# Two attention layers on one core: the first pair of heads, one ordering instruction earlier, one product later, one table load earlier

## The chip, the cores and the metric

The kernel runs on one core of one Trainium2 chip. The time is the device time of the whole program in microseconds (us), as the median of several runs. All data are 32-bit floats.

## What is computed

The input x has 4 images of 32x32 positions and 768 channels. Two layers are applied, each `x = x + attention(groupnorm(x))`. Cut to one layer (the second has biases on q, k and v, and tables for 14x14 positions that are clamped outside):

```
xn  = (x - mean) / sqrt(var + eps)         # 32 groups of 24 channels, no scale or shift
q, k, v = split(xn @ Wqkv)                 # 12 heads of 64
bias[query, key] = q . Rh[hq - hk] + q . Rw[wq - wk]
attn = softmax(scale * q k^T + bias)       # 1024 x 1024 for each head and image
x   = x + (attn @ v) @ Wproj + bproj
```

## The kernel before, in words

**Tiling.** Channels lie on the 128 partitions, six chunks of them (`NC`), positions on the free axis, 1024 (`S`) in two halves of 512. Two heads make a pair: head 0 of the pair uses rows 0 to 63 of TensorE's array, head 1 rows 64 to 127. There are 8 images (4 for each layer) with 6 pairs each, so 48 pairs `g`. A pair has 8 units `n` of 128 queries each. A unit (g, n) makes the scores of 128 queries against 1024 keys for both heads.

**One unit's chain.** `biases` (L513) adds the two position terms on GpSimd into a tile `sc` (two instructions, one for each head). `scores` (L527) is four matmuls of 64x512 on TensorE into PSUM. `exponentials` (L540) adds the bias on VectorE with the row minimum (L546) and takes exp with the row sum on ScalarE (L550). `divide` (L555) takes a reciprocal on VectorE (L558), which has to wait until both exps have ended, and multiplies on ScalarE (L564) or, for one head in units 2 and 4, on GpSimd (L562). `turn` (L566) transposes on VectorE (L570), writes to DRAM, and a later read brings the transposed tile back as `pt`. `weigh` (L586) multiplies with the values. Six `sc` tiles exist, so the biases of unit n + 3 wait for the transposes of unit n. PSUM holds two score tiles (the two heads of one unit) and two tiles of 1024 for everything else.

**The products for the next pair.** While pair g runs, q and k of pair g + 1 are made by four products G0 to G3 (`products`, L347), and values for two pairs at a time by four products of kinds 0 to 3 (`values`, L409); two of these four are made in each pair, under the names V0 and V1. They are a block product with seven multiplications in place of eight, so sums and differences of tiles and of weights (on GpSimd: `combine`, L130, `combine_values`, L141, `sums`, L296) come ahead of them and VectorE additions behind.

**Crossed halves.** A product other than kind 3 is written in two halves (`crossed`, L332). In the first half head-row group 0 takes one operand and group 1 the other, in the second half they change over. Between the halves stands an ordering instruction (`Crossed.between`, L325): a reduction over one column of a weight tile onto itself on VectorE (L330), or a copy on ScalarE (L328). It reads and writes what the first half has read and the second half will read, so it waits for the first half, and the second half waits for it. It computes nothing new. Kind 3 (G3, L369; the value product of kind 3, L426) has no halves and no ordering instruction.

**Order.** The order on every engine is the order of the Python calls; each engine takes its own instructions strictly in that order. The loop over units (L828) puts into unit (g, n): the ordering instructions that are held, the biases of unit n + 2, the scores and exponentials of unit n + 1, the transposes of unit n, the reciprocal of unit n + 1 and its multiplications, and between them the products that the plan names for n (L820 to L824, `run_part`, L885). A first half that was begun puts its product into `held`; its ordering instruction comes at the next unit, except in units 2 and 6.

**The front.** Before the loop (L775 to L819) stand the norm of image 0 (`norm_first`, L214: sums over groups, a square root on ScalarE at L232, the normalization of twelve half chunks, alternately on VectorE, L241, and ScalarE, L239), all four products of q and k for pair 0, the value products of kinds 0 and 3 (V0 at L799, V1 at L808), the position terms (`positions`, L461; `place_positions`, L485, writes them to DRAM; `diagonals`, L498, reads them back skewed, eight DMAs for each half of the queries), then biases, scores, exponentials and the division of unit (0, 0), and the first half of G0 for pair 1, whose ordering instruction comes as the first thing of unit (0, 0). In pair 0 the DMAs of head 1 in `diagonals` are issued by ScalarE's queue (L506), all others by SyncE's.

Of the kernel before, what the change touches and what calls it, by code (L numbers as in the profile page):

```python
# [56 lines left out]
def attention_blocks(ctx: ExitStack, tc: tile.TileContext, a: dict, out: bass.AP):  # L57
# [156 lines left out]
    def norm_first():  # L214

        mv = mv_of[0]
        w = small.tile([P, 2, NC], FP, tag="nrm", bufs=2, name="nrm_work")
        nrm = small.tile([P, NC, 2], FP, tag="nrm", bufs=2, name="nrm_0")
        total = ps_m.tile([P, 2, HALF], FP, tag="m", name="groups_0")[:, :, 0]
        work = nrm.rearrange("p c s -> p (c s)")  # L220
        part, mean, inv, shift = (work[:, k : k + 1] for k in range(4))
        off, var = w[:, 0, :], w[:, 1, :]
        nc.vector.tensor_reduce(part, mv[:, :, 0], mybir.AxisListType.X, ALU.add)
        nc.tensor.matmul(total[:, 0:1], lhsT=same_group, rhs=part, start=True, stop=True)
        nc.vector.tensor_scalar(mean, total[:, 0:1], 1.0 / GS, None, ALU.mult)
        nc.vector.tensor_scalar(off, mv[:, :, 0], mean, None, ALU.subtract)
        nc.vector.tensor_tensor(var, off, off, ALU.mult)
        nc.vector.tensor_tensor(var, var, mv[:, :, 1], ALU.add)
        nc.vector.tensor_reduce(part, var, mybir.AxisListType.X, ALU.add)
        nc.tensor.matmul(total[:, 1:2], lhsT=same_group, rhs=part, start=True, stop=True)  # L230
        nc.vector.tensor_scalar(inv, total[:, 1:2], 1.0 / GS, EPS, ALU.mult, ALU.add)
        nc.scalar.activation(part, inv, AF.Sqrt)  # L232
        nc.vector.reciprocal(inv, part)
        nc.vector.tensor_scalar(shift, mean, inv, -1.0, ALU.mult, ALU.mult)

        def apply(c, h, scalar):
            x = xn_of[0][h][c]
            if scalar:
                nc.scalar.activation(x, x, AF.Identity, bias=shift, scale=inv)  # L239
            else:  # L240
                nc.vector.tensor_scalar(x, x, inv, shift, ALU.mult, ALU.add)  # L241

        return apply
# [254 lines left out]
    def diagonals(g, i):  # L498
        td = t_of[g]
        for h in range(2):  # L500
            for y in range(4):
                src = bass.AP(
                    td.tensor, td.offset + (4 * i * P + HW * y) * P + h * 2 * HW + HW - 1,
                    [[P - 1, HW], [P * P, 4], [1, HW]],
                )
                (nc.scalar if h and not g else nc.sync).dma_start(  # L506
                    out=rel_of[g, i][y * HW : (y + 1) * HW, h, 1, :, :], in_=src
                )

# [45 lines left out]
    def divide(g, n):  # L555
        st = st_of[g, n]
        last = g + 1 == NPAIR
        nc.vector.reciprocal(st[:, 2, :], st[:, 1, :])  # L558
        for h in range(2):
            sc = sc_of[g, n, h].rearrange("p k j -> p (k j)")  # L560
            if h == 0 and n in (2, 4) and not last:
                nc.gpsimd.tensor_scalar(sc, sc, st[:, 2, h : h + 1], 1.0, ALU.mult, ALU.mult)  # L562
            else:
                nc.scalar.mul(sc, sc, st[:, 2, h : h + 1])  # L564
# [209 lines left out]
    with tc.manual_schedule(engines=ENGINES):  # L774
# [30 lines left out]
            combine_values(0, stage)  # L805
        load_w(1, "a")
        now["G3"].part()
        now["V1"].part()  # L808
        positions(0, 1)()
        run(later)  # L810
        run(later)
# [1 line left out]
        fetch(3)  # L813
        biases(0, 0)
        scores(0, 0)()
        divide(0, 0)
        biases(0, 1)
        ahead["G0"].part()
        held = [ahead["G0"]]  # L819
        same = {  # L820
            0: ("O1 previous", "G0", "V0"), 4: ("G1", "G3", "G2"), 5: ("G2", "O0"),
            7: ("O0", "O1", "G0 next"),
        }
        plans = {**same, 1: ("V0", "V1"), 3: ("V1", "G1")}, {**same, 1: ("V0",), 3: ("G1", "V1")}  # L824
        before = {}

        units = [(g, n) for g in range(NPAIR) for n in range(NT)]
        for at, (g, n) in enumerate(units):  # L828
            im, pair = divmod(g, NP)
            end = im + 1 == NI  # L830
            if n == 0:
                now = dict(ahead) if g + 1 < NPAIR else {}
                ahead = prepare(g + 2) if g + 2 < NPAIR else {}
                if g + 1 < NPAIR:
                    now.update(out_groups(g))
                now["O1 previous"] = before.get("O1")
                now["G0 next"] = ahead.get("G0")
                before = now
                if pair == 3 and not end:
                    stages, apply = norm(im + 1)  # L840
                todo = []
                if g + 1 == NPAIR:
                    fetch_last()
                    todo = put_out(im, 0, range(8, 12)) + put_out(im, 1, range(12))
                    todo += put_out(im, 2, range(0, 12, 2))
            shares = [0, 3, 0, 4, 4, 3, 0, 4]
            if (pair, n) in loads and not end:
                load_x(im + 1, loads[pair, n], 0)
            if pair == 4 and n in (1, 2) and not end:
                for c in range(3 * n - 3, 3 * n):  # L850
                    load_x(im + 1, c, 1)
            if im + 1 < B:
                if pair == 0 and n < NC:
                    load_x(im + 1, n, 0, 1)
                c = n - 2 if pair == 0 else loads.get((pair, n - 2), loads.get((pair - 1, n + 6), -1))
                if pair < 3 and c >= 0:
                    stats(im + 1, c, 1 if pair == 0 else 0, xn_of[im + 1][0][c])
            if n == 3 and 0 < g + 1 < NPAIR - 1:
                later.append(lambda: load_w(g + 2, "a"))
            for group in held if n not in (2, 6) else ():  # L860
                group.between()
            if n not in (2, 6):
                held = []
            run(early)
            early, later = later, early
            if at + 2 < len(units):
                biases(*units[at + 2])
            exps = scores(*units[at + 1]) if at + 1 < len(units) else None
            if n == 7:
                placing = []  # L870
            if n == 7 and g + 1 < NPAIR:
                placing.append(positions(g + 1, 1))
            if exps:
                exps()
            if n in (2, 7):
                run(placing)
            run(behind[0])
            behind.append(behind.pop(0))
            if pair == 3 and n in stages and not end:
                stages[n]()  # L880
            pieces = [now[name] for name in plans[pair % 2].get(n, ()) if now.get(name)]
            if n == 0 and len(pieces) == 2:
                pieces.insert(0, None)

            def run_part(k):  # L885
                if k < len(pieces) and pieces[k]:
                    group = pieces[k]
                    started = group.parts is not None
                    group.part()
                    if not started and group.last is not None:  # L890
                        held.append(group)

            run_part(0)
            turn(g, n)
            done = 2 if n == 0 else len(pieces) if n == 1 or (n, pair % 2) == (3, 0) else 1
            for k in range(1, done):
                run_part(k)
            if n == 1:
                placing = [positions_of() for positions_of in early_positions]
                early_positions.clear()  # L900
            if (n, pair % 2) == (3, 0):
                for group in held:
                    group.between(scalar=True)
                held = []
            if at + 1 < len(units):
                divide(*units[at + 1])
            if n in (0, 1) and g + 1 < NPAIR:
                combine(g + 1, n)
            if n in (3, 5) and pair % 2 and g + 1 < NPAIR:
                combine_values(g + 1, n // 4)  # L910
            if pair == 4 and not end:
                for h, c in applies.get(n, ()):
                    apply(c, h)
            if not end:
                for which, c in sum_steps.get((pair, n), ()):
                    sums(im + 1, which, c)
            if (n, pair % 2) == (3, 1):
                for group in held:
                    group.between()
                held = []  # L920
            for k in range(done, len(pieces)):
                run_part(k)
            take(todo, shares[n])
            if n == 6:
                weigh(g, (0, 1))
            elif n == 2 and g:
                weigh(g - 1, (2, 3))
# [63 lines left out]
```

## Time and profile before

| What | us |
|---|---|
| Median of 3 runs | 3318.47 |
| Lowest and highest of them | 3314.69, 3321.06 |
| The profiled execution, its own time | 3317.58 |
| Its span, first to last instruction | 3315.3 |
| TensorE busy in it | 3270.6 (99%) |
| VectorE busy | 2549.7 (77%) |
| GpSimd busy | 2386.5 (72%) |
| ScalarE busy | 1999.1 (60%) |

In the views of the profile PE is TensorE's matmuls, PEld its weight loads, DVE VectorE, ACT ScalarE, POOL GpSimd, SP SyncE; a q behind the name is the engine's queue of control instructions and DMA issues. Times count from the start of the span. A row of the timeline has the start, the duration, the engine, the line and the operation, the tiles (out<-in) and the shape, the count, and in brackets the idle time of the engine before it with what ended it. The tile `pj` is the PSUM tile of a q/k product, `pv` of a value product, `tp` of a position product, `s` of scores, `av` of values weighed, `sm` the sums of a softmax. A 32-bit matmul is recorded as two; so a half of a q/k product is x12, and a half of a value product x48.

### The profile page before, as it was taken

To read this page: it belongs to the slowest core of one execution; us is meant where nothing else is said; L and a number is where in the kernel's file an instruction comes from. 1 tells how busy PE (TensorE), PEld (TensorE's weight loads), DVE (VectorE), ACT (ScalarE), POOL (GpSimd) and SP (SyncE) were. 2 spreads that over 40 slices of the span, in tenths; PEclk is the share of its full clock that TensorE was granted. 3 is DMA by queue.
4 is the path that set the end of the run, shared out by engine and by line. 5 is a ranking of instruction groups with operands and counts; after the bars stand their busy time and mean duration, and the time that the engine had idled before them with its cause. 6 is when DMAs were issued, how large, how long until landed. Compare 5 with 4: busy or idle time off the path is not lost.

```text
span 3315.3 us, 64963 instructions
## 1 busy us (share of the span) xinstructions
PE 3270.6 (99%) x25060; PEld 1882.7 (57%) x25060; DVE 2549.7 (77%) x4091; ACT 1999.1 (60%) x2996; POOL 2386.5 (72%) x1259
## 2 busy tenths in 40 slices
PE   7999999999999999999999999999999999999998
PEld 4566555655555555555555555655555555655554
DVE  5887778877787877777777777777777777777775
ACT  3676655566556665566655666566656567565653
POOL 6877866679676796667867778677786777767762
PEclk9999999999999999999999999999999999999999
DMA  4999899899998998899989999899998999898987
GB/s 134 329 343 316 315 339 330 316 336 322 331 318 316 329 330 307 317 328 319 334 308 316 330 321 329 313 327 316 334 322 304 338 317 331 311 327 299 329 287 269
DMA packets 524180, 1047.38 MB, mean 316 GB/s; under 512 B 139104, under 2 KB 202080, under 8 KB 474720
## 3 DMA queue, kind: packets, MB, share of 16 engines
q1 hardware_dynamic: 470976, 1015.84, 86.1%
q10 hardware_dynamic: 52896, 27.40, 2.8%
q8 instruction: 198, 3.24, 0.4%
q14 instruction: 110, 0.90, 0.1%
HBM read 568.00 MB, written 475.09 MB: 315 GB/s over the span
## 4 chain that ended last, share of the span: by engine, by line
PE 90%; DMA 5%; DVE 2%; POOL 1%; issue 1%; SPq 0%; ACT 0%; ACTq 0%; DVEq 0%; POOLq 0%
PE pj L341 21%; PE s L534 19%; PE av L599 18%; PE oo L341 13%; PE pv L341 11%; PE pj L369 3%; DMA td<-tb 3%; PE tp L472 2%; PE pv L426 2%; DMA pt<-td 1%; DMA xn<-in_x 1%; DVE tb L570 1%; PE o L678 1%; POOL sc L520 1%; DVE st L209 0%
## 5 line engine op out<-in xcount | busy, mean ns | idle before, releaser
L520 POOL TENSOR_TENSOR sc<-rel 128x1024 f32<-128x1024 f32 x768 | 1879.4, 2481 | 473.1 <-DVE tb L570 454.9
L546 DVE CUSTOM_DVE_ANT_0 sc<-s,sc 128x1024 f32<-128x1024 f32 x768 | 910.9, 1223 | 353.1 <-PE s L534 288.3
L564 ACT ACTIVATE sc<-sc,sm 128x1024 f32<-128x1024 f32 x674 | 743.5, 1144 | 643.2 <-DVE sm L558 494.5
L550 ACT ACTIVATE sc<-sc,sm 128x1024 f32<-128x1024 f32 x768 | 878.5, 1146 | 350.5 <-DVE sm L546 349.0
L570 DVE STREAM_TRANSPOSE tb<-sc 128x1024 f32<-128x1024 f32 x768 | 908.1, 1223 | 59.6 <-DMA td<-tb 55.7
L534 PE MATMUL s<-k,q 64*128 64x512 f32 x3072 | 738.8, 596 | 2.8 <-DVE sm L546 2.7
L599 PE MATMUL av<-pt,v 128*64 128x256 f32 x6144 | 686.2, 381 | 10.3 <-DMA pt<-td 9.0
L599 PEld LDWEIGHTS av<-pt,v 128*64 128x64 f32 x6144 | 436.7, 137 | 289.2 <-issue 49.2
L341 PE MATMUL oo<-attn,wo 64*128 64x512 f32 x2112 | 475.3, 589 | 0.0
L534 PEld LDWEIGHTS s<-k,q 64*128 64x128 f32 x3072 | 284.0, 187 | 302.7 <-issue 268.7
L562 POOL TENSOR_SCALAR sc<-sc,sm 128x1024 f32<-128x1024 f32 x94 | 105.9, 1127 | 374.9 <-DVE sm L558 374.9
L341 PEld LDWEIGHTS oo<-attn,wo 64*128 64x128 f32 x2112 | 201.1, 187 | 227.8 <-issue 226.9
L341 PEld LDWEIGHTS pv<-wv,xn 64*128 64x128 f32 x4608 | 271.6, 188 | 35.2 <-issue 25.1
L341 PE MATMUL pv<-wv,xn 64*128 64x128 f32 x4608 | 274.1, 272 | 1.0 <-DVE wv L330 1.0
L341 PE MATMUL pj<-xn,wa 64*128 64x512 f32 x1152 | 268.2, 596 | 5.1 <-DVE wa L330 3.5
L341 PE MATMUL pj<-xn,w 64*128 64x512 f32 x1152 | 263.4, 589 | 0.0
L341 PE MATMUL pj<-s,w 64*128 64x512 f32 x576 | 262.7, 589 | 0.6 <-DVE v L443 0.6
L341 PE MATMUL pj<-s,wc 64*128 64x512 f32 x576 | 262.7, 589 | 0.0
L341 PEld LDWEIGHTS pj<-xn,wa 64*128 64x128 f32 x1152 | 113.5, 189 | 140.5 <-issue 125.5
L341 PEld LDWEIGHTS pj<-xn,w 64*128 64x128 f32 x1152 | 112.5, 187 | 134.8 <-issue 132.9
L443 DVE TENSOR_TENSOR v<-pv,v 128x512 f32<-128x512 f32 x216 | 140.2, 686 | 61.0 <-ACT v L445 44.0
L495 ACT COPY rel<-raw 32x256 f32<-32x256 f32 x384 | 155.0, 404 | 11.3 <-DMA part<-res 3.4
(93 smaller groups left out, 2642.0 us busy)
## 6 DMA issues: line engine op xcount, KB each, us to landing
td<-tb SPq DMA_DIRECT2D x384, 1024.0 KB, 6.3
pt<-td SPq DMA_DIRECT2D x382, 1024.0 KB, 8.8
tdr<-t ACTq DMA_DIRECT2D x96, 256.0 KB, 6.2
part<-res SPq DMA_DIRECT2D x84, 256.0 KB, 4.4
res<-part SPq DMA_DIRECT2D x84, 256.0 KB, 4.8
wa<-in_wqk SPq DMA_DIRECT2D x48, 384.0 KB, 3.1
wc<-in_wqk SPq DMA_DIRECT2D x48, 384.0 KB, 6.9
wv<-in_wv SPq DMA_DIRECT2D x24, 768.0 KB, 12.6
```

The lines of the kernel that those rows point to most:

```text
L341: nc.tensor.matmul(to, lhsT=w, rhs=x, start=at == half == 0, stop=at == 0 and half == 1)
L369: nc.tensor.matmul(t[:, h, :], lhsT=w[rows, c, :], rhs=x[c][rows, :], start=(c == 0), stop=(c == NB - 1),)
L443: add = lambda to, x, y: nc.vector.tensor_tensor(to, x, y, ALU.add)
L495: nc.scalar.copy(rel[rows, :, 0, :, :], raw[rows, :, :, WIDE - 1 - HW - y : WIDE - 1 - y])
L520: nc.gpsimd.tensor_tensor(sc.rearrange("p (a k) (u l) -> p a (k u) l", a=4, l=8), rel[:, h, 0, m, :].unsqueeze(1).unsqueeze(3).to_broadcas ...
L534: nc.tensor.matmul(ps[h][:, cols], lhsT=q[rows, n * P : (n + 1) * P], rhs=k[rows, cols], start=True, stop=True,)
L546: nc.vector.tensor_tensor_reduce(out=sc, in0=ps[h], in1=sc, scale=-scale, scalar=BIG, op0=ALU.add, op1=ALU.min, accum_out=st[:, 0, h : h + 1],
L550: nc.scalar.activation(sc, sc, AF.Exp, bias=st[:, 0, h : h + 1], scale=-1.0, accum_out=st[:, 1, h : h + 1],)
L562: nc.gpsimd.tensor_scalar(sc, sc, st[:, 2, h : h + 1], 1.0, ALU.mult, ALU.mult)
L564: nc.scalar.mul(sc, sc, st[:, 2, h : h + 1])
L570: nc.vector.transpose(tb[:, :, h, :], sc_of[g, n, h])
L599: nc.tensor.matmul(av[rows, at * 2 * P : (at + 1) * 2 * P], lhsT=v_of[g][:, k, rows], rhs=pt_of[g, quarter].rearrange("p n r k h i -> p (n ...
```

## The change

Five edits, all in the front or in pair 0:

1. In `norm_first`, behind the last step of the norm, one exponential of one column (`part` from `shift`, with scale 0). It brings ScalarE's load of the table of exponentials to this place; the result is not used.
2. In `diagonals`, the four DMAs of head 1 for the second half of the queries of pair 0 go to SyncE's queue; those of the first half stay on ScalarE's.
3. The value product of kind 3 for pair 0 leaves the front and goes into unit (0, 0), behind G0, under the name V3.
4. G0 of pair 1, first half, and its ordering instruction now both stand in front of the division of unit (0, 0), so in front of its reciprocal on VectorE.
5. The value products of pair 0's loop move one slot: V0 from units 0 and 1 to 1 and 2, V1 from 1 and 3 to 2 and 3. Unit (0, 2) no longer leaves out the ordering instruction.

```diff
         nc.vector.tensor_scalar(shift, mean, inv, -1.0, ALU.mult, ALU.mult)
+        nc.scalar.activation(part, shift, AF.Exp, scale=0.0)
...
-                (nc.scalar if h and not g else nc.sync).dma_start(
+                (nc.scalar if h and not g + i else nc.sync).dma_start(
...
         now["G3"].part()
-        now["V1"].part()
         positions(0, 1)()
...
         scores(0, 0)()
+        ahead["G0"].part()
+        ahead["G0"].between()
         divide(0, 0)
         biases(0, 1)
-        ahead["G0"].part()
-        held = [ahead["G0"]]
+        held = []
...
-        before = {}
+        first_plan = {
+            **same, 0: ("G0", "V3"), 1: ("V0",), 2: ("V0", "V1"), 3: ("V1", "G1"),
+        }
+        before = {"V3": now["V1"]}
...
-                now["O1 previous"] = before.get("O1")
+                now["O1 previous"], now["V3"] = before.get("O1"), before.get("V3")
...
-            for group in held if n not in (2, 6) else ():
-                group.between()
-            if n not in (2, 6):
+            if n not in (2, 6) or at == 2:
+                for group in held:
+                    group.between()
                 held = []
...
-            pieces = [now[name] for name in plans[pair % 2].get(n, ()) if now.get(name)]
+            pieces = [now[name] for name in (plans[pair % 2] if g else first_plan).get(n, ()) if now.get(name)]
```

The number of matmuls, of activations of full size, of transposes and of DMAs stays; one activation of one column is added. Behind pair 0 the order is that of before.

## The prediction, made before the changed kernel was run

> **What bounds the kernel now.** I read the page's busy shares first, then the waits of TensorE, then the chain of work and the timeline in the front, where all five edits lie.
>
> ```profile
> span 3315.3 us, 64963 instructions
> PE 3270.6 (99%) x25060; PEld 1882.7 (57%) x25060; DVE 2549.7 (77%) x4091; ACT 1999.1 (60%) x2996; POOL 2386.5 (72%) x1259
> ```
>
> TensorE is busy for all but 45 us, so only work or idle time of TensorE can be won. The loop behind the front is not touched; what TensorE is ahead at the end of pair 0 it keeps, if nothing else is late. Where does it idle in the front? The timeline of PE:
>
> ```profile
> 55.33 2.15 PE L534 MATMUL s<-k,q 64*128 64x512 f32 x8
> 60.46 4.54 PE L341 MATMUL pj<-xn,wa 64*128 64x512 f32 x12 [2.97 <-DVE wa L330]
> ...
> 78.79 3.13 PE L534 MATMUL s<-k,q 64*128 64x512 f32 x8 [1.43 <-DVE sm L546]
> 82.91 2.95 PE L341 MATMUL pv<-wv,xn 64*128 64x128 f32 x48 [0.99 <-DVE wv L330]
> ```
>
> Second half of G0 for pair 1: 2.97 us idle for the ordering instruction, then 4.4 us (60.46 to 64.83, where the next product starts) for what takes 2.57 elsewhere (52.76 to 55.33). The table by stretch says why the half was slow (the column 0.50 is the granted clock):
>
> ```profile
> 61.40:64.70 3.30, 3.30 (x10) 1.39 (x8) 3.30 (x6) 3.01 (x5) 0.69 (x1) 0.50 0.33 127
> ```
>
> The clock was halved behind the idle time. So this stall cost 2.97 + 1.8 = 4.8 us. The chain of work shows what led to it:
>
> ```profile
> 51.88 2.31 DMA tdr<-t
> 54.22 0.36 ACTq L506
> ...
> 56.05 1.28 ACT L550
> 57.35 2.38 ACT sc L550 x4
> 59.79 0.46 issue
> 60.25 0.16 DVE wa L330
> ```
>
> ScalarE waits for the write of the position terms, issues four DMAs, loads the table of exponentials (1.28), does both exps; then comes the reciprocal, and only behind it on VectorE the ordering instruction, though its product's first half ended at 55.33.
>
> [...] half clock for 3.41 us after 2.97 idle. [...] The load is 1283 here[...] (the exp follows at 57.35, and the 2.08 us ahead of the load hold the DMA issues). [...] Identity and copies run behind exps without another load. [...] Here that is 4 x 0.45 = 1.8 us of ScalarE.
>
> **The change, step by step** (times of before's span, start cost left out until the end). I carry rows forward with before's durations: a q/k half product 2.57, a value half product 2.7, scores 1.72, position products 0.9; on VectorE a pair of L546 2.35, transposes 2.3; 0.2 from the end of a product to VectorE.
>
> *V3 leaves the front.* In before it ran from 47.39 to 50.14. Now the position products run from 47.4 to 48.3. Scores (0,0) need the last addition to k, which ends at 49.04 (47.62 + 1.42): V3 hid that, now PE idles 0.8. Scores 49.1 to 50.85, first half of G0 to 53.4, scores (0,1) to 55.2.
>
> *Ordering instruction.* VectorE does the L546 of (0,0) from 51.15 to 53.5, then the ordering instruction at 53.65 (0.2 after the half product). The second half of G0 follows the scores without idling: 55.25 to 57.8. The stall and the halved clock go. The wait that it adds: the reciprocal stands behind it. But the reciprocal is due only after the exps, and those: position copies from 48.5 to 51.2, no DMAs, no table, exps 52.35 to 54.85. Nothing is late by it. V3 then 57.8 to 60.6.
>
> *What is late next is VectorE.* From scores (0,1), at 55.5: L546 2.4, transposes (0,0) 2.3, addition to q 1.1, reciprocal 0.15, V3's two additions 1.4 (moved here), L546 of (0,2) 2.35: 65.1. Then transposes 2.3, reciprocal 0.1, statistics (L209) 0.65; the ordering instruction of V0 at 68.2 to 68.35. PE meanwhile: scores (0,2) to 62.3, V0's first half to 65.0, position products to 65.9, scores (0,3) to 67.6. It idles 0.8, and V0's second half runs from 68.4 to 71.1. V1's first half needs a PSUM tile; in the built order it takes that of the position products, free by 67.3, not that of V0. To 73.8; scores (0,4) to 75.5. VectorE: L546 of (0,3) to 70.65, V0's additions 71.3 to 73.2, transposes to 75.5, reciprocal, statistics, ordering instruction 76.25 to 76.4. PE idles 0.95; V1's second half 76.45 to 79.1.
>
> Before, V1's second half ended at 85.69, where G1 starts; from there both kernels have the same order, and before had no further idle time up to 107.7. **Gain: 85.69 - 79.13 = 6.6 us.** As a check, the losses that go: 2.97 + 1.8 + 1.43 + about 1.2 (the 3.13 of the scores) + 0.99 = 8.4, less new ones of 0.8 + 0.8 + 0.95 = 2.55, leaves 5.9; 0.7 are small gaps between rows.
>
> *Covers.* GpSimd: biases (0,3) start after the transposes of (0,0), 59 to 64; VectorE wants them at 68.4. Biases (0,4) are ready at 75.6, wanted at 76.4. That cover is thin: without it each us costs one. DMAs: SyncE takes eight instead of four (3.5 us in place of 1.75), but starts 2.75 earlier, so weights, residual and image loads behind them are issued at 55 to 58 as before (56 to 58.9); position terms of the second half are needed at 70.7.
>
> *Start cost.* The built program puts the table load behind the norm's `shift` (ready at 19.01), with a wait: load 1.28 and the exponential 0.2 delay ScalarE's normalizations by 1.5. TensorE needs the first of them at 20.62, so from about 22.1. Until 23.8 its rate is half (a weight load per 0.85 us, later per 0.43), so if the clock rises at the same moment only 0.4 is lost[...]. Bounds 0.4 and 2.2[...]. [...] 0.4 + 0.43 x 1.7 = **1.1**. That shift reaches 47.4 whole, since the waits between (34.44, for VectorE's addition to v) move along with it.
>
> *Sum.* 6.6 - 1.1 = 5.5. Against the profiled execution, 3317.58: 3312.1. The median of the runs is 0.9 above that execution: 3318.47 - 5.5 = **3313.0**.
>
> **The rivals.**
>
> A. The forecast, 3313.0. Chance 0.60.
>
> B. The front's gain is collected again by DMAs. For: DMA engines are busy 0.95 from 105 to 170, and TensorE waits for `pt` at 107.75 (0.24) and 165.4 (2.24). Against: the chain into 108.0 starts at the transposes of (0,3), which move 6.5 earlier too. If half is given back: 3318.47 - 2.8 = 3315.7. Chance 0.17.
>
> C. More is won: the clock rises in time (0.4), and the 2.24 us at 165.4 vanish as the transfers fall otherwise. 6.6 - 0.4 + 2.2 = 8.4: 3310.1. Chance 0.17.
>
> D. Slower. In unit (0, 2) the ordering instruction of V0 stands on VectorE behind the statistics (L209), which wait for the image load, and that load stands on SyncE behind eight position DMAs now. Issued at about 58.9 as before, it has to land by 68.6. Loads of `xn` took 6.4 (chain at 90.47) and 10.11 (at 147.11). All gain is gone if it takes over 15.3 (5.5 more than the 9.8 of slack). With 20 us TensorE would stall from 68.7 to 79, past the 3 us that halved its clock: 10.3 + 1.8 above the forecast, 3325.1. Chance 0.06: three 1 MB moves would have to come ahead of it.
>
> That the load of the table isn't moved at all is excluded by the built order: no second one ahead of the first exp.
>
> **How the numbers follow.** 0.2% (6.6 us) is about what a measurement here can tell from no change; the forecast lies 1.1 us inside. Faster by more: C's 0.17 and a fifth of A (start cost near its low end, runs spread over 6 us): 0.30. Slower: most of D, 0.05. Within: 0.65. Range: below, 3318.47 - 6.6 + 0.4 - 2.2 = 3310.1, and 0.6 for the spread: 3309.5. Above, B with 1.8 where executions of before don't all halve the clock: 3317.5.
>
> **What would show it.** Right: no idle time near 57; clock 1.0 from 48 to 105; idle of about 0.8, 0.8, 0.95 ahead of scores (0,0), V0's and V1's second halves; G1 of pair 1 first half at about 80 (85.69 before). Wrong: TensorE's first q/k product more than 2.2 late; statistics in unit (0, 2) waiting for `xn`; L546 of (0,4) waiting for POOL; idle before `av` at 102 over 1 us.

## The result, and the profile after

The changed kernel takes 3313.17 us (median of 19 runs, 3310.29 to 3319.63) against 3320.10 for the kernel before (19 runs, 3312.12 to 3324.23). The ratio is 0.9983, with a 95% interval of 0.9977 to 0.9990: 0.17% faster, 5.6 us of 3320, with an interval of 3.3 to 7.6 (the two medians lie 6.9 apart, the two means 5.5). The forecast was 5.5 us and 3313.0. That the median fell within 0.2 of it is in part luck: the kernel before came out 1.6 above the 3318.47 from which the forecast was counted.

The profiled execution took 3317.11 us, with a span of 3314.9, only 0.4 below the span before. That is one execution of a program whose times spread over 9 us; where its gain went is looked at below. The front can be read instruction by instruction in it. Page and timeline of PE:

```profile
span 3314.9 us, 64967 instructions
PE 3271.2 (99%) x25060; PEld 1884.7 (57%) x25060; DVE 2548.7 (77%) x4091; ACT 1998.0 (60%) x2997; POOL 2385.2 (72%) x1259
```

```profile
51.25 1.99 PE L535 MATMUL s<-k,q 64*128 64x512 f32 x8 [0.53 <-DVE k L386]
...
55.64 2.15 PE L535 MATMUL s<-k,q 64*128 64x512 f32 x8
57.36 3.01 PE L342 MATMUL pj<-xn,wa 64*128 64x512 f32 x12
...
70.32 2.95 PE L342 MATMUL pv<-wv,s 64*128 64x128 f32 x48 [0.26 <-DVE wv L331]
...
78.22 2.95 PE L342 MATMUL pv<-wv,xn 64*128 64x128 f32 x48 [0.55 <-DVE wv L331]
```

The second half of G0 (57.36) follows its scores without idle time, and the next product starts 2.57 later: the stall of 2.97 and the halved clock (0.50 from 61.33 to 64.74 before) are gone. Three small waits stand in their place, where they were forecast: for the last addition to k (0.53), for the ordering instructions of V0 (0.26) and V1 (0.55). The stretch where the clock had been halved now has 1.00 in its column:

```profile
61.40:64.70 3.30, 3.30 (x41) 3.03 (x40) 3.27 (x6) 1.67 (x4) 3.01 (x2) 1.00 0.91 246
```

ScalarE's timeline shows both ends of the moved load. At the norm it pushes the normalizations (L240); in front of the exps (L551) ScalarE now idles:

```profile
18.56 1.28 ACT L235 ACT_TABLE_LOAD   x1 [0.53 <-DVE nrm L234]
19.85 0.20 ACT L235 ACTIVATE nrm<-nrm 128x1 f32<-128x1 f32 x1
19.96 4.33 ACT L240 ACTIVATE xn<-xn,nrm 128x512 f32<-128x512 f32 x6
...
54.65 1.15 ACT L551 ACTIVATE sc<-sc,sm 128x1024 f32<-128x1024 f32 x1 [1.20 <-DVE sm L547]
```

TensorE's start pays for the first of these. The first row is the kernel before, the other two are the changed kernel:

```profile
19.65 4.93 PE L341 MATMUL pj<-xn,wa 64*128 64x512 f32 x11 [1.51 <-DVE xn L241]
...
19.11 2.07 PE L342 MATMUL pj<-xn,wa 64*128 64x512 f32 x2 [1.51 <-DVE xn L242]
21.52 4.63 PE L342 MATMUL pj<-xn,wa 64*128 64x512 f32 x9 [0.34 <-ACT xn L240]
```

**Two marks.** Single executions differ by more than the change is worth, so I compare two stretches that lie on the path. S runs from the start of the norm's `shift` on VectorE to the first matmul of G1 of pair 0: 18.80 to 34.44 before, 18.26 to 36.59 after. A runs from there to the first matmul of G1 of pair 1: to 85.69 before, to 81.00 after. The rows, before and then after:

```profile
18.80 0.21 DVE L234 TENSOR_SCALAR nrm<-nrm 128x1 f32<-128x1 f32 x1
34.44 0.66 PE L341 MATMUL pj<-s,w 64*128 64x512 f32 x1 [0.60 <-DVE v L443]
85.69 0.59 PE L341 MATMUL pj<-s,w 64*128 64x512 f32 x1
...
18.26 0.21 DVE L234 TENSOR_SCALAR nrm<-nrm 128x1 f32<-128x1 f32 x1
36.59 0.66 PE L342 MATMUL pj<-s,w 64*128 64x512 f32 x1 [0.60 <-DVE v L444]
81.00 0.59 PE L342 MATMUL pj<-s,w 64*128 64x512 f32 x1
```

A repeats well: it is 44.40 to 44.44 in the changed kernel and in experiments 1, 2, 3 and 10, which all come to the same waits there. S moves by up to 1.4 between executions of one order, for a reason given below. Each kernel has one trace, the kernel before too.

| us | S | A | rest of TensorE's work |
|---|---|---|---|
| before | 15.64 | 51.26 | 3225.8 |
| changed | 18.33 | 44.41 | 3230.1 |

A is 6.85 shorter, S is 2.69 longer. The rest, from G1 of pair 1 to the end of the last matmul, has the same order in both kernels and took 4.2 longer in this execution. So three questions stay: what of the five edits made the 6.85, what the 2.69 are, and whether the 4.2 belong to the change.

### The profile page after: what moved, and what is told of

The parts are those of the page before. It is cut to its first block, busy times and chain, and to the rows that moved or that the text cites. A ratio compares the mean times of both kernels' runs of the same rounds, so it can differ in the third digit from the quotient of the medians.

```text
span 3314.9 us, 64967 instructions
## 1 busy us (share of the span) xinstructions
PE 3271.2 (99%) x25060; PEld 1884.7 (57%) x25060; DVE 2548.7 (77%) x4091; ACT 1998.0 (60%) x2997; POOL 2385.2 (72%) x1259
## 4 chain that ended last, share of the span: by engine, by line
PE 89%; DMA 7%; DVE 2%; issue 1%; POOL 1%; SPq 1%; ACT 0%; DVEq 0%; POOLq 0%; ACTq 0%
PE pj L342 21%; PE s L535 18%; PE av L600 18%; PE oo L342 13%; PE pv L342 11%; DMA td<-tb 4%; PE pj L370 3%; PE tp L473 2%; PE pv L427 2%; DMA pt<-td 1%; DVE tb L571 1%; PE o L679 1%; DMA xn<-in_x 1%; POOL sc L521 1%; DMA xn<-mid 0%
## 5 line engine op out<-in xcount | busy, mean ns | idle before, releaser
L551 ACT ACTIVATE sc<-sc,sm 128x1024 f32<-128x1024 f32 x768 | 878.5, 1146 | 343.9 <-DVE sm L547 342.4
L600 PE MATMUL av<-pt,v 128*64 128x256 f32 x6144 | 686.5, 381 | 11.5 <-DMA pt<-td 10.2
```

The source lines that it names most:

```text
L551: nc.scalar.activation(sc, sc, AF.Exp, bias=st[:, 0, h : h + 1], scale=-1.0, accum_out=st[:, 1, h : h + 1],)
L600: nc.tensor.matmul(av[rows, at * 2 * P : (at + 1) * 2 * P], lhsT=v_of[g][:, k, rows], rhs=pt_of[g, quarter].rearrange("p n r k h i -> p (n ...
```

## The experiments

The theory is that of the prediction: the stall came from the ordering instruction that stood behind the reciprocal, VectorE in strict order is bound next, and the table load delays TensorE's start. The rivals are that ScalarE's late exps made all of it (then the place of the ordering instruction is nothing), and that the start depends only on the moment at which the clock rises. Every kernel was timed against the kernel before on the same chip; medians are given with the median of before in the same runs.

**1. Without the load at the norm.**

```diff
-        nc.scalar.activation(part, shift, AF.Exp, scale=0.0)
```

> The changed kernel without its first edit, so the table of exponentials loads ahead of the first exp of unit (0,0) again. Two marks in the trace: S, from the norm's shift to the first matmul of G1 of pair 0 (before 15.6, changed 18.3), and A, from there to the first matmul of G1 of pair 1 (before 51.3, changed 44.4). My theory (the load delays TensorE's start; in unit (0,0) it only pushes the reciprocal by 1.3, of which 0.84 is idle time of VectorE): S back to 15.6, A 44.4 + 0.5 = 44.9, median 0.5 to 2 us under the changed kernel. Rival (the load in front of the exps is what made the stall): S 15.6, A 45.7 or more, with TensorE idle ahead of the second half of G0; median not under the changed kernel.

Measured: S 16.66, A 44.40; 3309.65 against 3319.18, ratio 0.9977 (0.9968 to 0.9986). S falls, and A doesn't rise by the 0.5 that I had expected. ScalarE's timeline in this kernel tells why:

```profile
50.91 1.66 ACT L495 COPY rel<-raw 32x256 f32<-32x256 f32 x4 [0.15 <-ACT raw L480]
52.59 1.28 ACT L550 ACT_TABLE_LOAD   x1
53.89 1.15 ACT L550 ACTIVATE sc<-sc,sm 128x1024 f32<-128x1024 f32 x1
```

The load didn't wait for the data of the exp that follows. It started at 52.59, when the copies ended, and was over at 53.87; VectorE delivered the first row minima at 53.72. So all but 0.15 of it lay in the time that ScalarE idles there in the changed kernel (1.20 us). In the changed kernel the first edit costs 1.7 in S, by these two traces, and brings nothing in A.

**2. The ordering instruction behind the reciprocal again.**

```diff
         ahead["G0"].part()
-        ahead["G0"].between()
         divide(0, 0)
+        ahead["G0"].between()
```

> The changed kernel with the ordering instruction of G0 behind the reciprocal of unit (0,0) again; all else stays. If the place of the instruction is what took the stall away: TensorE idle near 57 comes back, A over 46. If the exps, now early by the table and the four DMAs, made the stall go, its place is worth nothing here: the reciprocal ends at 57.2, TensorE is with scores (0,1) until 57.4, A 44.4 to 44.6. I expect the second. [...]

Measured: S 17.88, A 44.41; 3313.80 against 3319.18, ratio 0.9983 (0.9975 to 0.9991). The place is worth nothing here. VectorE's timeline, and TensorE's row of the second half of G0: the reciprocal (L559) is done early enough.

```profile
56.23 0.17 DVE L559 RECIPROCAL sm<-sm 128x2 f32<-128x2 f32 x1 [1.31 <-ACT sc L551]
56.31 0.15 DVE L331 TENSOR_REDUCE wa<-wa 128x1 f32<-128x1 f32 x1
...
56.52 3.01 PE L342 MATMUL pj<-xn,wa 64*128 64x512 f32 x12
```

TensorE asks for it at 56.5, when the scores (0,1) are through. This half of my theory, that the place of the instruction is what removes the stall, falls for the changed kernel.

**3. The load in ScalarE's idle time.**

```diff
-        nc.scalar.activation(part, shift, AF.Exp, scale=0.0)
...
+        def load():
+            nc.scalar.activation(part, shift, AF.Exp, scale=0.0)
...
                 apply(c, h, c % 2 == 1)
+        load()
```

> The changed kernel with the exponential of one column moved behind the twelve normalizations, where ScalarE has 8 us of idle time. My theory: S 15.6 as in before, A 44.4 as in the changed kernel; so 1 to 2.7 us under the changed kernel in the front, the median near 3311.5. Rival (the start cost comes from something else, as the phase of the clock alone): S stays between 16 and 18.3.

Measured: S 15.73, A 44.41; 3309.79 against 3319.18, ratio 0.9973 (0.9965 to 0.9982). As expected, S of before with A of the changed kernel. The load runs behind the last normalization, where ScalarE is then idle for 5.49 us:

```profile
23.02 1.28 ACT L244 ACT_TABLE_LOAD   x1
...
30.01 0.58 ACT L396 COPY q<-pj 128x512 f32<-128x512 f32 x1 [5.49 <-PE pj L344]
```

With experiment 1 it is the best version run: both medians lie 3.4 to 3.5 under the 3313.17 of the changed kernel, of which 0.9 is the lower median of before in these runs (3319.18 for 3320.10); the intervals of the ratios overlap. A closer comparison is experiment 2, timed on the same chip, which has the load at the norm and the same A: its mean is 3.7 above that of experiment 3, with an interval of 2.2 to 5.2 from resampling both sets of runs.

**4. Four position DMAs on ScalarE's queue again.**

```diff
-                (nc.scalar if h and not g + i else nc.sync).dma_start(
+                (nc.scalar if h and not g else nc.sync).dma_start(
```

> The changed kernel with the second half's four position DMAs on ScalarE's queue again. They wait for the write of the position terms to land and take 1.8 us, so exps (0,0) start about 3 later (57.6 in place of 54.65) and the reciprocal at 60.0. My theory (VectorE in strict order is the next bound): scores' first VectorE step of (0,1) goes from 58.1 to 60.2, A 44.4 + 2.1 = 46.5. Rival (ScalarE's lateness is covered): A 44.4 to 44.8.

Measured: S 18.10, A 46.92; 3316.86 against 3319.18, ratio 1.0000 (0.9992 to 1.0009). The second edit is worth 2.5 us by A, and without it the ratio can't be told from nothing. ScalarE:

```profile
51.59 1.66 ACT L496 COPY rel<-raw 32x256 f32<-32x256 f32 x4 [0.15 <-ACT raw L481]
55.51 1.81 ACTq L507 DMA_DIRECT2D rel<-tdr  x4
57.37 1.15 ACT L551 ACTIVATE sc<-sc,sm 128x1024 f32<-128x1024 f32 x1 [4.12 <-issue]
```

Not the 1.81 of issuing is the larger part, but the time from 53.25 to 55.51 in which the queue waits for the position terms' write to land (issued at 51.16, landed 4.3 later). The prediction counted only the 1.8.

**5. From before: the ordering instruction in front, alone.**

```diff
         scores(0, 0)()
+        ahead["G0"].part()
+        ahead["G0"].between()
         divide(0, 0)
         biases(0, 1)
-        ahead["G0"].part()
-        held = [ahead["G0"]]
+        held = []
```

> The kernel before with the fourth edit alone: first half of G0 and its ordering instruction in front of the division of unit (0,0). My theory (the ordering instruction behind the reciprocal made the stall at 57.5, VectorE is bound next): the 2.97 us and the halved clock go, but exps, reciprocal and so scores' VectorE steps stay late; A (from the first matmul of G1 of pair 0 to that of pair 1; before 51.3) falls to 48.0. Rival (ScalarE's lateness is what counts): A over 50. S as before, 15.6 to 16.7.

Measured: S 16.20, A 48.27; 3316.88 against 3319.86, ratio 0.9994 (0.9986 to 1.0003). The mark says 3.0 us, as expected; the medians alone couldn't have told it. Of the 3.0, 1.8 are the halved clock that is gone. The idle time moves from 57 to a place further on:

```profile
55.82 2.15 PE L534 MATMUL s<-k,q 64*128 64x512 f32 x8
57.54 3.01 PE L341 MATMUL pj<-xn,wa 64*128 64x512 f32 x12
...
66.62 2.95 PE L341 MATMUL pv<-wv,s 64*128 64x128 f32 x48 [1.68 <-DVE wv L330]
```

**6. From before: the load alone, in ScalarE's idle time** (the edit of experiment 3, made in the kernel before).

> The kernel before with only the load of the table of exponentials taken to ScalarE's idle time behind the normalizations. The exps, the reciprocal and the ordering instruction come 1.3 earlier; the idle time at 57.5 falls to 1.6 and no longer halves the clock (1.8). My theory: A 47.9. If the halved clock stays: A 49.5. Rival (the load is covered here as it was in the changed kernel): A 51.

Measured: S 16.85, A 48.30; 3315.15 against 3319.86, ratio 0.9987 (0.9981 to 0.9994). Near 47.9, and the clock stays up:

```profile
60.38 2.85 PE L344 MATMUL pj<-xn,wa 64*128 64x512 f32 x12 [1.70 <-DVE wa L333]
```

So in the kernel before, where the exps follow the DMA issues without a pause, the same 1.28 us are worth 3.0: 1.27 of idle time and 1.8 of halved clock. Behind these 1.70 us of idle time the half product took 2.68 (60.38 to 63.06), behind the 2.97 of before 4.37.

**7. From before: load and DMA queue** (the edit of 6 and the change's second edit).

> The kernel before with the load in ScalarE's idle time and the four DMAs on SyncE's queue: exps (0,0) from 54.3, the reciprocal at 56.8, the ordering instruction at 57.0, before TensorE asks for it (57.4). My theory: no stall there, A 46.4, though no instruction was put in front of the reciprocal; what is left against 44.4 is the place of the value products. Rival (the place of the ordering instruction is needed): idle time at 57 stays, A over 49.

Measured: S 15.76, A 46.58; 3312.70 against 3319.86, ratio 0.9979 (0.9970 to 0.9988). The stall at 57 is gone but for 0.4 us (scores take 1.72, so TensorE asks at 56.39), with every instruction of VectorE in its old place:

```profile
54.67 2.15 PE L537 MATMUL s<-k,q 64*128 64x512 f32 x8
56.79 2.85 PE L344 MATMUL pj<-xn,wa 64*128 64x512 f32 x12
```

Either early exps or the early ordering instruction remove that stall, all but 0.4 of it; not both are needed. Early exps are worth 1.7 more (4.7 against 3.0), because they also bring reciprocal and transposes forward.

**8. From before: the value products moved, alone** (third and fifth edits).

```diff
-        now["V1"].part()
...
+        first_plan = {
+            **same, 0: ("G0", "V3"), 1: ("V0",), 2: ("V0", "V1"), 3: ("V1", "G1"),
+        }
...
```

> The kernel before with the third and fifth edits alone: the single value product goes into unit (0,0), V0 and V1 one slot on; load, DMA queue and ordering instruction as before. The exps of unit (0,0) come 2.75 earlier, but scores (0,1) and the second half of G0 too, so the stall for the ordering instruction stays, about 2.0. My theory: A 44.4 + 1.8 = 46.2, or 47.9 if the clock halves again. Rival (the product only filled a stall, or the gain is all in the other edits): A 50 or more.

Measured: S 16.17, A 49.42; 3318.38 against 3319.86, ratio 0.9996 (0.9988 to 1.0005). A miss by 1.5 to 3.2. The stall was 3.33, not 2.0, and the clock halved again (0.50 from 58.9 to 61.7):

```profile
58.81 4.26 PE L341 MATMUL pj<-xn,wa 64*128 64x512 f32 x12 [3.33 <-DVE wa L330]
```

```profile
49.06 0.38 ACTq L487 DMA_DIRECT2D tdr<-t  x1
...
52.98 1.81 ACTq L506 DMA_DIRECT2D rel<-tdr  x4
```

The write of the position terms, issued at 49.06, let the next DMAs go after 3.92 us; before it took 2.34 (51.88 to 54.22). Without V3 it is issued 1.6 us behind a weight load of 384 KB (SyncE, 47.45), before 4.3 us behind it (47.61). The same holds in all traces: with V3 in the front the next DMAs went 2.3 us after the write (four traces), without it 2.9 to 4.7 (eight). That the load holds the write back is my reading; no run separates it from other effects of the move.

**9. The same, with the ordering instruction in front.**

```diff
+        ahead["G0"].part()
+        ahead["G0"].between()
         divide(0, 0)
         biases(0, 1)
-        ahead["G0"].part()
-        held = [ahead["G0"]]
+        held = []
```

> The kernel with the value products moved alone (third and fifth edits), and the fourth edit added: first half of G0 and its ordering instruction in front of the division. There the late write of the position terms left a stall of 3.3 us for the ordering instruction and a halved clock, A 49.4. My theory: with the instruction in front both go, but the reciprocal still comes at 24.3 after the first G1, so scores' VectorE steps are as late as with the four DMAs on ScalarE's queue, plus 0.85: A 47.8. Rival (the instruction's place is worth nothing, as it was with early exps): A 49.4.

Measured: S 15.45, A 48.34; 3315.68 against 3318.34, ratio 0.9991 (0.9983 to 0.9999). A is 1.1 us less than in experiment 8, half a microsecond short of the expectation. The stall is gone and the clock stays up (the half product takes 2.57, 54.48 to 57.05), but the reciprocal, now with TensorE's later products behind it, gives waits further on:

```profile
64.91 2.95 PE L341 MATMUL pv<-wv,s 64*128 64x128 f32 x48 [1.43 <-DVE sm L558]
...
71.36 2.95 PE L341 MATMUL pv<-wv,s 64*128 64x128 f32 x48 [0.90 <-DVE wv L330]
```

In experiment 8 the half product after the stall took 4.10 (58.81 to 62.91) instead of 2.57. So the halved clock accounts for 1.5, more than the whole 1.1: apart from the clock, these two traces show no gain from the place of the instruction with late exps. Whether it has one is left open, since the write held the DMAs back 0.6 longer here (48.50 to 52.98) than in experiment 8.

**10. Three table loads at the norm.**

```diff
         nc.scalar.activation(part, shift, AF.Exp, scale=0.0)
+        nc.scalar.activation(part, shift, AF.Sqrt, scale=0.0)
+        nc.scalar.activation(part, shift, AF.Exp, scale=0.0)
```

> The changed kernel with two more one-column activations behind the first, a square root and an exponential again, so that ScalarE loads three tables there in place of one: 3.0 us more ahead of its normalizations. My theory (the start cost is the delay of ScalarE's normalizations, passed on whole): S 18.1 + 3.0 = 21.1, A 44.4 unchanged, median 3.0 above the changed kernel, 3316. Rival (the start cost is the phase of the clock, which rises at the same moment anyway): S under 19.5.

Measured: S 21.55, A 44.44; 3315.85 against 3318.34, ratio 0.9991 (0.9982 to 0.9999). TensorE waits for ScalarE, and the start cost grows with the delay:

```profile
25.03 4.63 PE L344 MATMUL pj<-xn,wa 64*128 64x512 f32 x9 [3.36 <-ACT xn L242]
```

3.0 more of ScalarE gave 3.45 more of S over the 18.10 that is the mean of the three kernels with one load there.

## Why the prediction was right, point by point

**The gain in the front** was 6.6 by the working and 6.85 by the mark A. The working put new waits of 0.8, 0.8 and 0.95 into it; they were 0.53, 0.26 and 0.55. Of both numbers 1.8 are the clock that halved in the one trace of the kernel before. Other waits of 2.24 (before, at 165.41) and 2.87 us (experiment 9, at 1779.43) had full clock behind them, so other executions of before may lack those 1.8; how many do was not shown. The mean gain in A then lies somewhere from 5.05 to 6.85 (an estimate: the 6.85 of the traces without and with the 1.8).

**Where the stall went.** The working said of the ordering instruction in front of the reciprocal that the stall and the halved clock go. They went, but experiment 2 shows that in this kernel they go without it, since three other edits make the reciprocal early. The working even had the numbers for that (exps until 54.85, TensorE asking at 55.25) and didn't draw the conclusion. From before, alone, the edit is worth 3.0 (experiment 5).

**The exps.** "no DMAs, no table" was right for the DMAs (2.5, experiment 4) and wrong for the table in this kernel (0, experiment 1): there it would have been loaded in ScalarE's idle time. The load alone, put into idle time, is worth 3.0 in the kernel before (experiment 6). The edits don't add up: 3.0 for the ordering instruction, 3.0 for the load and 1.8 for the value products alone, 4.7 for load and queue together, 6.85 for all. The first two and the 4.7 each contain the same 1.8 of halved clock. The value products are worth 2.2 once the exps are early: A is 46.58 in experiment 7 and 44.41 in experiment 3, and the ordering instruction, in which the two also differ, is worth nothing there (experiment 2).

**VectorE is late next.** Right. Once the stall is gone, reciprocal and transposes set A: with exps 2.9 later, counted from G1 of pair 0 (experiment 4), A grows by 2.5.

**The start cost** was 1.1 by the working, with bounds of 0.4 and 2.2. That the clock could rise later, and in 43% of executions, was my estimate; the trace of before doesn't show it. In eight kernels without a load at the norm S is 15.45 to 16.85, 16.06 in the mean; in three with one it is 17.88 to 18.33, 18.10 in the mean. So the term is 2.0, 0.9 more than predicted, and the one pair of traces in the table (2.69) lies over the upper bound. The trace's record of the granted clock splits it. The clock rose 4.60 to 7.43 after `shift` in the eight (4.98 in before, 7.43 in experiment 6) and 8.04 to 8.95 in the three. Take half of this time from S, since TensorE's rate is half until then (before: a q/k matmul of one row group each 0.85 us up to 23.78, each 0.43 behind it): what is left is 13.13 to 13.15 in all eight, 13.85 to 13.86 in the three, and 15.36 with three loads. So the spread of S without a load is the moment of the rise, and the cost has two parts.

The first is what a load costs if the clock rises at the same moment: 0.71, where the working had 0.4. ScalarE's delay of 1.5 falls into a time at half rate, so by the working's own numbers it should have been half of 1.5. Three loads, a delay of 4.5, cost 2.21, again half. The second is the later rise: 2.67 later in the mean of the three, half of which is 1.3, where the working had 0.7. Three executions are too few to say whether the 43% was wrong or these rises came late by chance. The gain in A was taken 0.25 too low and this cost 0.9 too low; by the marks the forecast of 5.5 was 0.7 too high.

**The covers.** GpSimd's biases were never waited for by unit (0, 4). The image load was issued at 62.31, not at 58.9 as I had it: the front as a whole stood 2.15 later (G1 of pair 0 at 36.59 for 34.44), and the write ahead of the position DMAs took 2 us longer to land (51.37 to 55.75, for 51.88 to 54.22); the statistics in unit (0, 2), at 69.54, still didn't wait. But the three image loads of that stretch took 5.5 to 8.7 to land, so the first can't have been there before 67.8. The working gave the load 9.8 us to land before rival D begins; it had 7.2, of which at most 1.7 were to spare. Rival D didn't come, and was nearer than I had it.

**Rival B, the gain collected again later.** The profiled execution looks like it: 4.2 longer behind the front. But in the twelve traces of this study the same stretch took 3220.3 to 3231.0, mean 3226.1, standard deviation 2.9, whatever stands in the front; experiments 1 to 3, with the same front in A, had 3223.9, 3227.4 and 3225.7. The waits for `pt` differ by execution (9.0 us in all in the trace of before, the longest 2.2; 10.2 and 1.9 in that of the changed kernel). So the 4.2 lie within that spread and need nothing of the change, and the run times agree: 6.85 - 2.0 = 4.85 by the marks (an estimate from 3.05 up, if the clock halves in only a part of the executions of before), 5.6 (3.3 to 7.6) by the ratio. Of rival C, the clock did not rise in time (8.95 after `shift`, for 4.98 before). The wait of 2.24 at 165.4 is not in the changed kernel's execution, but with nearly the same order behind the front there is 2.26 at 163.9 in experiment 4 and 2.20 at 160.8 in experiment 2, so this too differs by execution.

## What to carry to other kernels

Cover decides what an instruction costs, not its length: 1.28 us of table load were worth 3.0 in one order (1.8 of it through the clock) and 0 in another, and cost 1.7 to 2.7 where the loaded engine had been the next one wanted. Look for the engine's idle time and put the load there; before adding a second remedy for one stall, ask whether the first has removed it. And where a change is near 0.2%, measure it in the trace between two marks on the bound engine: A repeated to 0.04 where whole times spread over 10 us. A mark that spans a change of the clock, as S does, repeats only when that is taken out (13.13 to 13.15 in eight kernels, for 15.45 to 16.85).

## What was not expected of the hardware

The length of a wait of TensorE did not say whether its clock halved behind it: waits of 2.16 and 2.26 us were followed by a halved clock, one of 2.87 was not. Nine waits of these traces, by length, with the granted clock recorded behind each:

| Kernel | Idle, us from the span's start | Length | Granted clock behind it |
|---|---|---|---|
| experiment 8 | 55.48 to 58.81 | 3.33 | 0.50 |
| before | 57.48 to 60.46 | 2.97 | 0.50 |
| experiment 9 | 1779.43 to 1782.30 | 2.87 | 1.00 |
| experiment 6 | 1784.47 to 1787.20 | 2.73 | 0.50 |
| experiment 6 | 133.63 to 136.36 | 2.73 | 1.00 |
| experiment 4 | 163.90 to 166.16 | 2.26 | 0.50 |
| before | 165.41 to 167.65 | 2.24 | 1.00 |
| experiment 10 | 164.60 to 166.77 | 2.16 | 0.50 |
| experiment 8 | 164.97 to 166.87 | 1.90 | 1.00 |

Each of the five stretches of half clock lasted 3.41 us, and between the first rise and the last matmul the twelve traces have no other: none of it stood behind a wait shorter than 2.16. A stretch cost about 1.7 us (an estimate: half of 3.41; in before the half product took 1.8 longer, 4.37 for 2.57). So a wait of about 2.2 us was followed by that loss in two executions (2.26 in experiment 4, 2.16 in experiment 10) and by none in another (2.24 in before). What decides between them is left open here.
